# Closing a softmax in column halves and moving the output projection behind it, in a hand-ordered attention stage

## The chip, the cores and the metric

The kernel runs on one core of a Trainium2 chip. The metric is device time in microseconds (us), the median over runs. A core has five engines that run side by side and meet at semaphores: TensorE (PE in the profile; its weight loads are PEld), VectorE (DVE), ScalarE (ACT), GpSimd (POOL) and SyncE (SP, which issues DMAs).

## The reference, cut to what matters

The program is a network of four layers on 2708 tokens of 256 features. The change concerns one part of layer 2, a causal attention ahead of a mixture of experts:

```
h = rmsnorm(x, ln1_w)
q, k, v = h @ wq.T, h @ wk.T, h @ wv.T          # 4 query heads, 2 key/value heads, 64 wide
q, k = rope(q), rope(k)
scores = q @ k.T / 8 ; scores = where(causal, scores, -1e30)
y = softmax(scores) @ v
x = x + y @ wo.T                                # the output projection
flat = rmsnorm(x, ln2_w)
probs = softmax(flat @ router_w.T)              # the two best of 8 experts per token
out = sum over the two experts of weight * (silu(flat @ w1.T) * (flat @ w3.T)) @ w2.T
x = x + out
```

## The kernel before, in words

`attention` cuts the 2708 query columns into six blocks (`cols`): five of 512 (n = 0 to 4) and one of 148 (n = 5). Keys come in tiles of 128. A block has two pairs of heads, p = 0 and p = 1; both key/value heads of a pair are worked on side by side in the two halves of the partitions. In the last block both pairs are done as one, with m = 2 and 296 columns in all. One *step* (n, p, j) is a block, a pair and a key tile j. Causality lets block n see 4(n+1) key tiles, so that early pairs are short: 4, 8, 12, 16 and 20 steps. Two steps make a *group*.

What a step does:
- `scores` (L1913): TensorE multiplies queries and keys into a PSUM tile `sc`, two of which exist. ScalarE takes the exponential of it into an SBUF tile `e` (L1922); the first `e` of a pair is the tile `sum`. There are four `e` tiles. On the diagonal VectorE multiplies a 128-column part by a triangle, `upper` (L1928).
- `values` (L1938), one group later: TensorE adds `V` times `e` into the PSUM tile `po` of the pair, and VectorE adds `e` to `sum` (L1944).
- `close`, once per pair, one group after its last `values`: TensorE sums `sum` over the partitions with a matrix of ones into a PSUM tile `pd` (L1952), VectorE takes the reciprocal of all 512 columns into `yt` (L1954) and multiplies it by `po` (L1955).

Two generators run beside these steps and hand out work in pieces:
- `projects` (`heads`) prepares the next block: normalised rows `f` (VectorE, L124), their transposes `tp` (L1857, copied by ScalarE into `ft`), the values `pv`, and keys and queries in three pieces `pj` (L1884), each followed by two VectorE products with the rotation table (L1887) and an add on POOL (L1888). Behind the last block it frees its pool and starts the loads of the experts' weights. A counter `at` paces it: some 18 steps' worth of pieces per step of the block.
- `sends` (`tails`) takes up a block when both its pairs are closed (`closed`), one block after the other: two token tiles at a time it multiplies `yt` by `wo` into `wy` (the matmul at L139, in `matmul_k`; per tile one product for each pair), adds the normalised row to it (`xa`, L1970), adds that to the residual X on POOL (L1971), squares it on ScalarE (L1973), scales it (`h`, L1978), transposes it, computes the router's logits `pr`, and then, in `route.chunk`, picks the two experts of each token (a chain of small VectorE operations that ends in `dtaken` and `dso_far`), ranks the tokens with two small matmuls `rank` (L1569, L1570), and scatters each row to its two experts with indirect DMAs on POOL's queue (L1590), eight per block of 512 columns.

The PSUM tiles `tp`, `pv`, `pj`, `pd`, `wy`, `pr` and `rank` all come from one pool, `aux`, with two buffers. A piece that needs a buffer waits for whoever last reads what is in it.

TensorE's order is written out by hand (`manual_schedule`): it takes its instructions in the order in which the Python loop below issues them. The other engines' orders come from a scheduler. Per group the loop issues the scores of the group, one piece of `sends`, the values of the group before, the closes that are due, and then pieces of `projects` until the counter is satisfied:

```python
                for step in group:
                    exp = scores(*step)
                next(tails, None)
                for step in before:
                    values(*step)
                ...
                for n, p in ending:
                    close(n, p)
                ...
                while group and at[2] * ... < at[1] * 18:
                    at[2] += 1
                    next(heads, None)
```

After the last close the experts' stage (`mixture`, in `experts`) follows. Its matmuls (`h` at L2125) take the rows that the scatters have placed.

Of the kernel before, what the change touches and what calls it, by code (L numbers as in the profile page):

```python
# [12 lines left out]
ALU = mybir.AluOpType  # L13
# [3 lines left out]
P = 128  # L17
# [18 lines left out]
def rows(t):  # L36
    return min(P, N - t * P)
# [11 lines left out]
def tiles_of(start, length):  # L49
    return range(start // P, (start + length + P - 1) // P)  # L50
# [282 lines left out]
def inverse_root(net, pool, v, scale, eps, name, out=None):  # L333


    nc = net.nc
    n = v.shape[1]
    x = pool.tile([P, n], F32, name=f"{name}x")
    nc.vector.tensor_scalar(x, v, scale, eps, ALU.mult, ALU.add)
    half = pool.tile([P, n], I32, name=f"{name}h")  # L340
    nc.vector.tensor_scalar(half, x.bitcast(I32), 1, None, ALU.logical_shift_right)
    y = pool.tile([P, n], F32, name=f"{name}y") if out is None else out
    nc.vector.tensor_scalar(y.bitcast(I32), half, -1.0, float(0x5F3759DF), ALU.mult, ALU.add)
    t = pool.tile([P, n], F32, name=f"{name}t")
    for _ in range(3):
        nc.vector.scalar_tensor_tensor(t, y, -0.5, y, ALU.mult, ALU.mult)
        nc.vector.tensor_tensor(t, t, x, ALU.mult)
        last = nc.vector.scalar_tensor_tensor(y, t, 1.5, y, ALU.add, ALU.mult)
    return y if out is None else last
# [1436 lines left out]
def attention(net, route, ln2, router, weights, mixture):  # L1786
# [7 lines left out]
    nc, tc, a, X = net.nc, net.tc, net.a, net.X  # L1794
# [3 lines left out]
    with ExitStack() as ctx:  # L1798
# [39 lines left out]
        queries, results = {}, {}  # L1838
# [51 lines left out]
        def by_pairs(t, m, iw):  # L1890

            return t[..., : m * iw].rearrange("p (m i) -> p m i", m=m)
# [4 lines left out]
        outs, sums, es = {}, {}, {}  # L1897
# [48 lines left out]
        def close(n, p):  # L1946
            iw = cols[n][1]
            m = queries[n][p].shape[1]
            e = sums.pop((n, p))
            pd = aux.tile([P, 512], F32, name="pd", tag="aux")  # L1950
            for g, b in enumerate(halves):
                nc.tensor.matmul(pd[b, : m * iw], net.ones[:, :DH], e[:, g, : m * iw], start=True, stop=True)  # L1952
            y = results[n][:, p : p + m, :iw]
            nc.vector.reciprocal(y, by_pairs(pd, m, iw))  # L1954
            nc.vector.tensor_tensor(y, y, by_pairs(outs.pop((n, p)), m, iw), ALU.mult)  # L1955

        def send(n, rp, aux, tag="aux"):
            i0, iw = cols[n]
            its = tiles_of(i0, iw)
            yt = results.pop(n)  # L1960
            ss = rp.tile([P, 4], F32, name="ss")
            nc.vector.memset(ss, 1.0)
            xs, hs = {}, {}
            for k, t in enumerate(its):
                r = rows(t)
                po = aux.tile([P, D], F32, name="wy", tag=tag)
                net.matmul_k(po[:r], yt[:, :, k * P : k * P + r], wo)
                xa = xs[t] = rp.tile([P, D], F32, name="xa", bufs=len(its))
                net.normed(xa, t, ln)
                nc.vector.tensor_tensor(xa[:r], po[:r], xa[:r], ALU.add)  # L1970
                nc.gpsimd.tensor_tensor(X[:r, t, :], X[:r, t, :], xa[:r], ALU.add)  # L1971
                h = hs[t] = rp.tile([P, D + 2], F32, name="h", bufs=len(its) + 1)
                nc.scalar.activation(h[:r, :D], xa[:r], AF.Square, accum_out=ss[:r, k : k + 1])  # L1973
                if k % 2 or tag != "aux":
                    yield
            for k, t in enumerate(its):
                r, h = rows(t), hs[t]
                nc.vector.tensor_tensor(h[:r, :D], xs[t][:r], ln2[:r], ALU.mult)  # L1978
            if tag != "aux":
                yield  # L1980

            root = inverse_root(net, rp, ss, 1.0 / D, 1e-6, "rr")
            yield
            for k in range(0, len(its), 2):
                pair = its[k : k + 2]
                ps = aux.tile([P, 2, 2 * P], F32, name="tp", tag=tag)
                for m, t in enumerate(pair):
                    r, h = rows(t), hs[t]
                    for c in range(2):
                        nc.tensor.transpose(  # L1990
                            ps[:, c, m * P : m * P + r], h[:r, c * P : (c + 1) * P], net.ident[:r, :r]
                        )
                nw = (len(pair) - 1) * P + rows(pair[-1])
                ht = rp.tile([P, 2, 2 * P], F32, name="ht")
                nc.scalar.copy(ht[:, :, :nw], ps[:, :, :nw])
                yield
                pr = aux.tile([P, 2, 8], F32, name="pr", tag=tag)
                for m, t in enumerate(pair):
                    r = rows(t)
                    net.matmul_k(pr[:r, m, :], ht[:, :, m * P : m * P + r], router)  # L2000
                for m, t in enumerate(pair):
                    r = rows(t)
                    nc.vector.tensor_scalar(
                        route.logits[:r, t, :], pr[:r, m, :], root[:r, k + m : k + m + 1], None, ALU.mult
                    )
                yield
            for k, t in enumerate(its):
                r, h = rows(t), hs[t]
                nc.vector.tensor_scalar(h[:r, :D], h[:r, :D], root[:r, k : k + 1], None, ALU.mult)
            yield from route.chunk(rp, aux, its[0], len(its), hs.__getitem__, tag=tag)  # L2010
# [8 lines left out]
        def projects():  # L2019
            for n in range(1, len(cols)):  # L2020
                while at[0] + 1 < n:
                    yield
                yield from (last_project if n + 1 == len(cols) else project)(n)
                ready.append(n)
                yield

        def sends():
            for n in range(len(cols) - 1):
                while n not in closed:
                    yield  # L2030
                yield from send(n, rp, aux)

        ready, closed, ending, at = [0], [], [], [0, 0, 0]
        with tc.manual_schedule(engines={mybir.EngineType.PE}):
            for _ in project(0):
                pass
            steps = [
                (n, p, j)
                for n, (i0, iw) in enumerate(cols)
                for p in range(2 if n + 1 < len(cols) else 1)  # L2040
                for j in range(tiles_of(i0, iw)[-1] + 1)
            ]
            groups = [steps[k : k + 2] for k in range(0, len(steps), 2)]
            heads, tails, before = projects(), sends(), []
            for group in groups + [[]]:
                while group and group[-1][0] not in ready:
                    next(heads)
                if group and group[0][0] > at[0]:
                    at[:] = group[0][0], 0, 0
# [4 lines that stand above are left out]
                    values(*step)  # L2054
                if at[0] + 1 == len(cols):
                    next(tails, None)
                for n, p in ending:
                    close(n, p)
                    if p + 1 == len(queries[n]):
                        closed.append(n)  # L2060
                ending = [(n, p) for n, p, j in before if j == tiles_of(*cols[n])[-1]]
                at[1] += 1
                while group and at[2] * len(queries[at[0]]) * (tiles_of(*cols[at[0]])[-1] + 1) < at[1] * 18:
                    at[2] += 1
                    next(heads, None)
                before = group
            for n, p in ending:
                close(n, p)
            for _ in tails:
                pass  # L2070
# [379 lines left out]
```

## Time and profile before

| what | value |
|---|---|
| median of 3 runs | 2646.69 us (2646.11 to 2649.6) |
| profiled execution, its own time | 2647.78 us |
| its span, first to last instruction | 2646.0 us |
| mean granted clock of TensorE | 0.962 |
| attention stage | about 1560 to 1945 us from the span's start |
| experts of layer 2 | from about 1945 us |
| reciprocals of closes, L1954 | 10 of 512 columns (3350 ns), 1 of 296 (2007 ns) |

The profile's windows give the busy time of each engine in a stretch of the span, with the granted TensorE clock; a matmul of the program appears as two passes in the trace, so `x8` at `wy` is two token tiles. The list of waits says who waited for whom: total us, number of waits, longest. In the timeline each row is a run of like instructions with its start and its length; idle time before it and what ended it stand in brackets. A group of instructions "by form" has the shape, the count, the busy time in us and the mean in ns.

### The profile page before, as it was taken

How to read it: one execution, taken by the hardware profiler on the slowest of the kernel's cores; microseconds unless marked ns; L12 is line 12 of the kernel's file. 1: busy time of each engine (PE TensorE's matmuls, PEld its weight loads, DVE VectorE, ACT ScalarE, POOL GpSimd, SP SyncE). 2: the span in 40 equal slices, each digit the busy share in tenths (PEclk: the TensorE clock that was granted, in tenths of full speed). 3: DMA queues.
4: the chain of work that ended last, by engine and by line, in shares of the span. 5: the costliest groups of instructions: out<-in, count | busy, mean ns of one | idle time of the engine just before them, and what ended most of it. 6: DMA issues, size and time to landing. Idle time of an engine off the chain costs nothing. (4 is left out here: it accounts for less than half of the span.)

```text
span 2646.0 us, 32568 instructions
## 1 busy us (share of the span) xinstructions
PE 2446.7 (92%) x11676; PEld 1581.2 (60%) x11676; DVE 1476.4 (56%) x3258; ACT 1060.2 (40%) x1714; POOL 329.2 (12%) x445
## 2 busy tenths in 40 slices
PE   5999999887999998979799989999899999969998
PEld 4666765574333334468578854444357777747887
DVE  7754348544788886333545457787653222264556
ACT  3444443313787772321434323334422222234454
POOL 1000002100000001134130011222231111110002
PEclk9999999978999999989899999999989999989999
DMA  8899520000000002774310010000231111050001
GB/s 289 281 299 320 172 86 31 3 6 1 1 1 1 1 1 82 170 193 144 91 62 1 1 38 9 19 17 17 101 128 50 33 33 33 22 203 7 1 1 43
DMA packets 106875, 197.70 MB, mean 75 GB/s; under 512 B 8846, under 2 KB 63736, under 8 KB 103876
## 3 DMA queue, kind: packets, MB, share of 16 engines
q1 hardware_dynamic: 88010, 146.82, 17.8%
q0 software_dynamic: 14896, 43.89, 5.1%
q10 hardware_dynamic: 3806, 4.85, 0.6%
q8 instruction: 98, 1.61, 0.3%
q14 instruction: 65, 0.53, 0.1%
HBM read 135.82 MB, written 59.71 MB: 74 GB/s over the span
## 5 line engine op out<-in xcount | busy, mean ns | idle before, releaser
L701 DVE SCALAR_TENSOR_TENSOR e<-e,mask 128x768 f32<-128x768 f32 (+3 forms) x352 | 417.0, 1215 | 241.9 <-ACT e L700 239.1
L700 ACT ACTIVATE e<-big_p,minus_one,ratio 128x768 f32<-128x768 f32 (+3 forms) x352 | 418.6, 1226 | 285.2 <-PE acc L1371 196.8
L1371 PE MATMUL acc<-V,e 128*128 128x257 f32 x1848 | 405.3, 382 | 5.7 <-DVE e L701 5.6
L1371 PEld LDWEIGHTS acc<-V,e 128*128 128x128 f32 x1848 | 352.7, 191 | 58.6 <-issue 7.0
L2125 PE MATMUL h<-w,ft 128*128 (+1 forms) x752 | 233.9, 452 | 1.3 <-DVE yl L1955 1.3
L307 PE MATMUL acc<-F,e 128*128 128x257 f32 (+1 forms) x924 | 212.5, 383 | 3.7 <-DVE e L303 3.4
L836 PE MATMUL acc<-e,V 128*64 128x512 f32 (+1 forms) x1056 | 209.1, 548 | 2.2 <-DVE e L701 2.2
L307 PEld LDWEIGHTS acc<-F,e 128*128 128x128 f32 (+1 forms) x924 | 171.6, 189 | 56.6 <-DVE e L303 29.2
L2142 DVE TENSOR_TENSOR hh<-hh,h 128x682 f32<-128x682 f32 x47 | 40.7, 865 | 243.7 <-PE h L2125 243.7
L2125 PEld LDWEIGHTS h<-w,ft 128*128 128x128 f32 x752 | 135.8, 191 | 57.2 <-issue 1.8
L836 PEld LDWEIGHTS acc<-e,V 128*64 128x64 f32 x1056 | 73.7, 138 | 151.3 <-issue 146.1
L1922 ACT ACTIVATE e<-sc 128x1024 f32<-128x1024 f32 (+4 forms) x131 | 107.1, 863 | 139.2 <-PE sc L1913 116.6
L303 DVE TENSOR_TENSOR e<-e,mask 128x512 f32<-128x512 f32 (+2 forms) x132 | 80.5, 621 | 141.3 <-ACT e L296 139.6
L1944 DVE TENSOR_TENSOR sum<-sum,e 128x1024 f32<-128x1024 f32 (+4 forms) x131 | 135.2, 1032 | 40.1 <-ACT e L1922 19.6
L296 ACT ACTIVATE e<-score 128x512 f32<-128x512 f32 (+2 forms) x132 | 69.4, 544 | 170.4 <-PE score L294 145.1
L2157 PE MATMUL po<-w,ht 114*128 (+1 forms) x564 | 131.5, 383 | 0.9 <-DVE ht L2150 0.9
L1913 PE MATMUL sc<-qt,kt 64*128 64x512 f32 (+5 forms) x568 | 123.9, 555 | 1.4 <-ACT sum L1922 0.9
L2157 PEld LDWEIGHTS po<-w,ht 114*128 114x128 f32 x564 | 107.6, 192 | 23.0 <-DVE ht L2150 8.2
L847 PE MATMUL den<-e,low 128*3 128x512 f32 (+1 forms) x1056 | 117.7, 542 | 0.0
L294 PE MATMUL score<-QK 128*128 128x512 f32 (+2 forms) x264 | 112.0, 553 | 3.4 <-ACT e L296 3.0
L1938 PE MATMUL po<-e,V 128*64 128x512 f32 (+5 forms) x524 | 111.2, 543 | 1.7 <-DVE e L1928 1.7
L2151 ACT COPY ht<-pt 114x256 f32<-114x256 f32 x47 | 17.5, 372 | 201.0 <-DVE ht L2150 201.0
(652 smaller groups left out, 3408.4 us busy)
## 6 DMA issues: line engine op xcount, KB each, us to landing
row<-in_adj SPq DMA_DIRECT2D x21, 1354.0 KB
raw<-in_adjT SPq DMA_DIRECT2D x35, 768.0 KB
hs<-zero SPq DMA_DIRECT2D x8, 2838.0 KB
hidden<-hr SPq DMA_DIRECT2D x32, 256.0 KB
wd<-in_f_wd SPq DMA_DIRECT2D x8, 1024.0 KB
kept<-mask SPq DMA_DIRECT2D x21, 338.5 KB
mask<-kept SPq DMA_DIRECT2D x21, 338.5 KB
w<-in_d_w1T SPq DMA_DIRECT2D x8, 682.0 KB
```

The costliest lines, as they stand in the source:

```text
L294: nc.tensor.matmul(ps[:r, :iw], QK[:, 0, span(j)], QK[:, 1, i0 : i0 + iw], start=True, stop=True)
L307: ended = nc.tensor.matmul(acc[k], e[:r, k * P : (k + 1) * P], F[:r, j, :], start=j == 0, stop=j == NT - 1)
L700: nc.scalar.activation(v, big_p[:, i], AF.Relu, bias=net.minus_one, scale=ratio)
L701: return nc.vector.scalar_tensor_tensor(v, v, 1.0, net.mask[:, j, i], ALU.add, ALU.mult)
L836: nc.tensor.matmul(acc[n][half, :iw], V[:, j, h, :], e[n][:, k, :iw], start=j == 0, stop=j == NT - 1)
L847: nc.tensor.matmul(den[g : g + Q, :iw], low[:, j, h, Q - 1 - q : 2 * Q - 1 - q], e[n][:, k, :iw], start=False, stop=j == NT - 1 and q == Q ...
L1371: nc.tensor.matmul(acc[k][:ri], e[:, k * P : k * P + ri], V[:, j, :], start=j == 0, stop=j == NT - 1)
L1913: nc.tensor.matmul(by_pairs(ps[:r, g], m, iw)[:, :, o:], kt[b, span(j)], qt[b, :, o:iw], start=True, stop=True)
L1938: nc.tensor.matmul(by_pairs(outs[n, p][b], m, iw)[:, :, o:], V[:r, j, g, :], by_pairs(e[:r, g], m, iw)[:, :, o:], start=j == 0, stop=j == ...
L1944: nc.vector.tensor_tensor(total, total, by_heads(e[:r], m, iw)[:, :, :, o:], ALU.add)
L2125: last = nc.tensor.matmul(halves[s, n][:, q, :HALF], fts[s][:, c, :], weights.w13[n][:, es[s], c, q * HALF : (q + 1) * HALF], start=c == 0 ...
L2157: last = nc.tensor.matmul(po, ht[:KP, k, :], w2[:KP, es[s], k, :], start=k == 0, stop=k == KC - 1)
```

## The change

Three edits, all in `attention`:
- `close` takes the reciprocal and the product in two column halves of 256 where m is 1. Where m is 2 it stays one piece.
- `sends` lets two of its turns pass after a block is closed, before it issues the first output projection. In the last block of the loop it has two turns per group, otherwise one.
- The pacing loop of `projects` is left early while `quiet` is above 0, that is in the group of a close and in the one after it, except while block 0 is worked on. Pieces held back are caught up afterwards, since the counter goes on.

```diff
@@ close
-            y = results[n][:, p : p + m, :iw]
-            nc.vector.reciprocal(y, by_pairs(pd, m, iw))
-            nc.vector.tensor_tensor(y, y, by_pairs(outs.pop((n, p)), m, iw), ALU.mult)
+            po = outs.pop((n, p))
+            half = 2 * P if m == 1 else iw
+            for i in range(0, iw, half):
+                y = results[n][:, p : p + m, i : i + half]
+                nc.vector.reciprocal(y, by_pairs(pd, m, iw)[:, :, i : i + half])
+                nc.vector.tensor_tensor(y, y, by_pairs(po, m, iw)[:, :, i : i + half], ALU.mult)
@@ sends
                 while n not in closed:
                     yield
+                for _ in range(2):
+                    yield
                 yield from send(n, rp, aux)
@@ the loop
-            heads, tails, before = projects(), sends(), []
+            heads, tails, before, quiet = projects(), sends(), [], 0
...
+                quiet -= 1
                 for n, p in ending:
                     close(n, p)
+                    quiet = 2
                     if p + 1 == len(queries[n]):
                         closed.append(n)
...
                 while group and at[2] * len(queries[at[0]]) * (tiles_of(*cols[at[0]])[-1] + 1) < at[1] * 18:
+                    if quiet > 0 and at[0]:
+                        break
                     at[2] += 1
                     next(heads, None)
```

## The prediction

> **What bounds the kernel now.** I read the windows first (busy time by stretch), then TensorE's waits inside the attention stage, then the timeline around one close, then the groups by form.
>
> ```profile
> PE 2446.7 (92%) x11676; PEld 1581.2 (60%) x11676; DVE 1476.4 (56%) x3258; ACT 1060.2 (40%) x1714; POOL 329.2 (12%) x445
> ...
> 1560.00:1945.00 385.00, 353.72 (x1634) 155.28 (x1633) 275.76 (x561) 142.06 (x211) 87.48 (x83) 0.95 0.11 36
> 1945.00:2160.00 215.00, 214.81 (x945) 157.08 (x946) 70.28 (x217) 46.36 (x107) 33.57 (x58) 0.99 0.19 63
> ```
>
> The second row is the stage changed, the third the expert stage behind it. TensorE (first number pair) works 354 of 385 us in attention, with a mean clock of 0.95, and without a gap afterwards; VectorE, 276 us, is next. So TensorE's issue order bounds the stage, and only its idle time, and the slow clock that follows it, can be won.
>
> ```profile
> PE wy L139 <- DVE yt L1955: 11.6, 4, 3.4
> PE pj L1884 <- DVE yt L1954: 5.9, 2, 3.6
> PE pj L1884 <- DVE xa L1970: 5.4, 1, 5.4
> ...
> PE pv L139 <- DVE xa L1970: 1.1, 1, 1.1
> ...
> DVE xa L124 <- POOL X L1971: 5.9, 1, 5.9
> ```
>
> Six gaps, 11.6 + 5.9 = 17.5 us, end with a reciprocal or its product: four where the output projection `wy` reads `yt`, two where a projection piece `pj` needs the PSUM tile that `pd` holds. The next two, 6.5 us, end with `xa`, because VectorE itself sat 5.9 us behind POOL. One close, that of query block 2, pair 1, in the timelines:
>
> ```profile
> 1718.85 1.03 PE L1952 MATMUL pd<-sum,ones 128*64 128x512 f32 x4
> 1719.81 0.66 PE L1857 MATMUL tp<-ident,f 128*128 128x128 f32 x4
> 1720.39 1.99 PE L1913 MATMUL sc<-qt,kt 64*128 64x512 f32 x8
> 1722.31 0.70 PE L139 MATMUL wy<-wo,yt 128*128 128x256 f32 x2
> 1725.82 2.23 PE L139 MATMUL wy<-wo,yt 128*128 128x256 f32 x6 [2.81 <-DVE yt L1955]
> 1727.98 2.91 PE L1938 MATMUL po<-e,V 128*64 128x512 f32 x8
> ```
> ```profile
> 1720.75 3.35 DVE L1954 RECIPROCAL yt<-pd 128x512 f32<-128x512 f32 x1
> 1724.02 1.16 DVE L1944 TENSOR_TENSOR sum<-sum,e 128x1024 f32<-128x1024 f32 x1
> 1725.09 0.68 DVE L1955 TENSOR_TENSOR yt<-yt,po 128x512 f32<-128x512 f32 x1
> ```
>
> `pd` ends at 1719.81 (call it T). The reciprocal starts at T+0.94, its product ends at T+5.96, and `wy` arrives at T+2.5. After the gap six passes took 2.23 us where an undisturbed `wy` takes 1.56, and the next `po` 2.91 for 1.94: another 1.64 us. By the same reading the six gaps (2.23, 2.36, 2.81, 3.40, 3.58, 3.13) are followed by 0, 1.83, 1.64, 2.86, 1.61 and 1.64 us of slow matmuls, 9.6 together, and the two POOL gaps (6.5) by 1.9. Removable at most: 17.5 + 9.6 + 8.4 = **35.5 us**.
>
> **What the Trainium skill says.** "TensorE: Matmul & The Clock Gate", Part 1: an idle window of about 3.4 us halves the array's clock, and it takes as long to return. The trace agrees on the halving, but 2.36 us of idle already cost 1.83; the measurement decides. The same page (engine queue depths) calls VectorE a strict FIFO: above, the product waits behind a `sum`. "Perfetto Trace Analysis", Optimizing Scalar/DVE Operations, advises breaking up an instruction that causes bubbles elsewhere, and puts some 125 ns of overhead on each with PSUM. That advice needs the pieces to be consumed separately; below they aren't.
>
> **The change part by part.**
>
> ```profile
> L1954 DVE RECIPROCAL yt<-pd 128x512 f32<-128x512 f32 x10 | 33.5, 3350 | 0.0
> ...
> L1954 DVE RECIPROCAL yl<-pd 128x296 f32<-128x296 f32 x1 | 2.0, 2007 | 0.7 <-PE pd L1952 0.7
> ```
>
> *Halves.* From the two rows, (3350 − 2007)/216 = 6.22 ns a column and 167 ns fixed; 256 columns cost 1759. The product (675 at 512, 461 at 296) is 421 for 256. A close pays 2 × (1759 + 421) − 4025 = 335 ns more, ten closes 3.35 us of VectorE; the last block (m = 2) has one piece and is unchanged. In the built program VectorE issues both half reciprocals and then both products, nothing between. So the first half of `yt` is ready at about T+0.94+3.4+0.4 = T+4.8, the second at T+5.2: against T+5.96 above little is won, and the `sum` adds of the next pair, which used to slip in between, come about 1.0 us later. By itself this part is worth between −0.3 us a close (product no longer behind a `sum`) and +0.3: I take 0. Its cover is TensorE's own work; where VectorE is late this is lost.
>
> *Output projection two groups later.* A group is 8 `sc` and 8 `po` passes, 1.92 + 1.87 = 3.8 us. Two of them put `wy` at T+9 or beyond, past T+5.2: at blocks 0, 2 and 3 its wait goes. In the last block a group takes 1.19 + 1.15, and `wy` moves by one: `wy` reaches its second matmul at about T+4.0 and waits till T+4.3. All of `send` moves along: per block 4 POOL adds of X, 4 squares on ScalarE, the routing chain, and 8 indirect DMAs on POOL's queue (about 1.3 us each, 10.4 in all). On SP's queue only the experts' weight loads behind the last projection move, some 8 us later against close (4,0); 80 us lie between that close and the experts, so I take 0, and up to 8 if that cover were gone. In the built order `rank` of block 0 now stands some 18 us of TensorE work ahead of block 1's `wy` instead of 2 groups: the 8 DMAs are through before the X adds queue, so the POOL gap (8.4 us) goes; I leave 0.5 for a `rank` that arrives as its chain ends.
>
> *No pieces beside a close.* `pj` no longer asks for `pd`'s buffer at T, so the waits of 2.36 and 3.58 go. Pieces are caught up in twos: at block 0/1, `tp`, `tp`, `pv`, `pj` stand in a row (0.3 us for ScalarE's copies). New orders to pay for, none seen in the trace of before:
> - close (0,1): `po` of the diagonal needs VectorE's `upper` behind the reciprocals: T+5.6 against T+4.5, 1.1 us.
> - close (1,0): `wy` of block 0 now stands just ahead. VectorE has `xa`, `h` (behind ScalarE) and next `xa` (behind POOL) before the reciprocal, which I put 2.5 us late: 3.5 us idle and slow matmuls of the size above. Between 0.7 and 5.5; I take 3.7.
> - close (2,0): `wy` one `sc` after `pd`, its second tile in `pd`'s buffer: T+4.4 against T+2.9, 1.5 us.
> - close (3,0): as (1,0), but it shows through the four `e` buffers: 0 to 5; I take 1.5.
> - close (4,0): second half of a `pj` behind `rank`'s buffer, 1.1; close (3,1): 0.3.
>
> The sum, us won: (0,1) 2.23 − 1.1 = 1.1; (1,0) 4.2 − 3.7 = 0.5; POOL gap 8.4 − 0.5 = 7.9; (2,0) −1.5; (2,1) 4.45; (3,0) −1.5; (3,1) 6.26 − 0.3 = 6.0; (4,0) 5.2 − 1.1 = 4.1. From (4,1) to the experts' first `tp` there are 44.5 us: 4.8 go with the gap, 0.3 stays, and the last 8 scatters, now one group nearer to the end, hold the experts' first load by up to 1: 4.2 taken. Together 25; I take off 3 for short waits in 8 reordered stretches that I can't place: **−22 us**. The stage behind starts earlier by the same amount: its TensorE has no gap, and its weight loads begin when attention's buffers close.
>
> The profiled execution took 2647.78 us (span 2646.0 and 1.8 around it), 1.1 above the median 2646.69. 2647.8 − 22 = 2625.8; for a median, **2625**.
>
> **Rivals.**
> - *VectorE's lag eats half.* In the sum the closes (1,0), (2,0), (3,0) keep 3.7 + 1.5 + 1.5 = 6.7 us of stall. If each costs 3.5 us idle and 1.7 slow, that is 15.6, 9 more: about −13, 2634. For it: VectorE is 72% busy in this stage, more beside `send`. Against it: close (2,0) and (3,0) had no gap before.
> - *Nothing moves.* The tight order only shifts waits to `rank` and `wy` slots: 2646. Against it: behind the closes (1,1), (2,0) and (3,0) stand `sc` and `po`, with at most a `tp` or `pr` between, as behind nearly all closes after the change, and TensorE had no gap there.
> - *Slower: the exp buffers.* ScalarE can't write the seventh `e` of a pair before VectorE has added the fourth, and `sc` can't go on before ScalarE has read its tile. From T: the add must end by about T+6.5; with the halves it ends at 0.94 + 4.2 + 1.14 = T+6.3, where before it was T+5.4. If the reciprocal starts later than T+1.1 at most closes, each us of lateness is a us of TensorE, and a slow clock comes with it. It ends slower by 5 once the ten closes lose over 3.4 us each (22 won + 6.7 counted + 5.3 = 34), that is with a lag over 2 us at every one: 2652 and up. Against it: at nine of the ten closes the reciprocal started 0.4 to 0.95 us after `pd`, once 1.6.
> - The change does what it says in the built order, the halves excepted, which is counted.
>
> **How the numbers follow.** 0.2% is 5.3 us, about what a measurement here tells from no change. Main case (−15 to −30): 0.68. Half eaten (−6 to −15): 0.18. Within 5.3: 0.06. Slower: 0.08. So faster 0.86. The range takes all but the last two and the unplaced rest: −34 (nearly all of 35.5) to −6, 2613 to 2641.
>
> **What would show it.** Right: no wait of `wy` on `yt` but in the last block; no `xa` wait of 5 us behind POOL; attention's clock at 0.98 or more; TensorE's idle time in the stage down from 31 to some 15 us; twenty reciprocals of 256 columns at about 1760 ns. Wrong: `po` or `sc` waiting on `upper` or `e` for over 2 us after most closes, or `rank` on `dtaken`.

## The result, and the profile after

The changed kernel took **2629.41 us** (median of 4 runs, 2627.47 to 2632.82) against 2648.07 for the kernel before on the same chip: a ratio of 0.9931, 95% interval 0.9919 to 0.9943. The forecast was 2625 in a range of 2613 to 2641. So the size came out near: 18.7 us won where 22 were forecast. The way there was not the one that I had described. In the profiled execution attention itself won about 31 us, and some 12 of them were given back in the first microseconds of the experts. (A second profiled execution, shown below, won 28 and gave back 2.)

The page's line of engines for the changed kernel, and then its windows; the columns of the rows are as before (TensorE, weight loads, VectorE, ScalarE, POOL, granted clock, DMA share, GB/s):

```profile
PE 2429.3 (93%) x11676; PEld 1575.1 (60%) x11676; DVE 1476.3 (56%) x3278; ACT 1060.7 (40%) x1714; POOL 326.6 (12%) x445
```
```profile
1560.00:1925.00 365.00, 338.96 (x1633) 150.17 (x1632) 275.69 (x583) 142.17 (x210) 85.00 (x83) 0.98 0.13 47
1925.00:2140.00 215.00, 214.29 (x940) 156.47 (x941) 69.97 (x215) 46.52 (x108) 32.56 (x57) 0.98 0.15 47
```

The stretch from the `wq` pieces of block 1 to the experts' first `h` is 19.0 us shorter (370.4 before, 351.3 after), with the same number of passes and the same work on VectorE. In the stage as a whole TensorE's busy time fell from 353.7 to 339.0 us for that work, and the mean clock rose from 0.95 to 0.98: this is slow clock that went. TensorE is still idle for 26 of the 365 us. Its waits in that stretch (total, number, longest):

```profile
PE tp L132 <- DMA f<-hs: 12.8, 1, 12.8
PE wy L139 <- DVE yt L1957: 3.2, 1, 3.2
PE rank L1569 <- DVE dtaken L1560: 2.2, 1, 2.2
PE pj L1884 <- DVE drank L1572: 2.0, 1, 2.0
PE po L1938 <- DVE e L1928: 1.9, 3, 0.8
```

The four waits of `wy` (11.6 us), the two of `pj` on `yt` (5.9) and the two on `xa` (6.5) are all gone. The 3.2 us of `wy` are new: they stand at close (2,0), where the kernel before had no gap. New too, and larger than any wait of the kernel before, is the first row: the experts' first transpose waits for the rows that the scatters have placed. The close of block 2, pair 1, once more in TensorE's and VectorE's timelines:

```profile
1708.11 1.03 PE L1952 MATMUL pd<-sum,ones 128*64 128x512 f32 x4
1709.07 1.99 PE L1913 MATMUL sc<-qt,kt 64*128 64x512 f32 x8
...
1711.97 1.94 PE L1938 MATMUL po<-e,V 128*64 128x512 f32 x8
```
```profile
1710.01 3.36 DVE L1957 RECIPROCAL yt<-pd 128x256 f32<-128x256 f32 x2
1713.29 0.69 DVE L1958 TENSOR_TENSOR yt<-yt,po 128x256 f32<-128x256 f32 x2
```

No idle time stands in brackets in TensorE's rows, and `po` takes the undisturbed 1.94 us where it took 2.91.

Now the seam to the experts in the timelines, with rows of POOL, of the queues of ScalarE and SP, and of TensorE. First the kernel before, then the changed one (in a row of a queue the second number is the time over which its DMAs were issued):

```profile
1935.90 1.51 POOL L1590 DMA_INDIRECT hs<-h,dto  x1 [0.30 <-DMA hs<-h,dto]
1940.75 1.31 ACTq L1712 DMA_DIRECT2D f<-hs  x3
1942.36 6.82 SPq L1460 DMA_DIRECT2D w<-in_d_w3T  x8
1942.99 0.66 PE L132 MATMUL tp<-ident,f 128*128 128x128 f32 x2 [0.18 <-DMA f<-hs]
```
```profile
1911.76 0.97 POOL L1590 DMA_INDIRECT hs<-h,dto  x1 [0.30 <-DMA hs<-h,dto]
1911.91 15.44 SPq L1460 DMA_DIRECT2D w<-in_d_w3T  x8
1917.82 1.34 ACTq L1712 DMA_DIRECT2D f<-hs  x3
1924.91 0.66 PE L132 MATMUL tp<-ident,f 128*128 128x128 f32 x2 [12.78 <-DMA f<-hs]
```

Before, the order was: last scatter, rows `f`, then the experts' weights `w3`. After, the weights are issued 0.15 us behind the last scatter and 5.9 us ahead of the first rows, because attention's buffers, which they go into, close just then: in all nine profiled executions with this order of loads they were issued 0.15 to 0.16 us after `so_many`, the last matmul of attention, began. The rows could be fetched only 6.1 us after the last scatter's issue, and needed 7.1 us to land, where they had needed 2.2. From 1912 to 1925 us the core's DMA engines were busy for 95% of the time (27% from 1905 to 1912). My theory from here on: **the weight loads get ahead of the scatters and of the rows**, and this costs what attention's last part had gained.

### The profile page after: what moved, and what is told of

The parts are those of the page before. It is cut to its first block, busy times and chain, and to the rows that moved or that the text cites. A ratio compares the mean times of both kernels' runs of the same rounds, so it can differ in the third digit from the quotient of the medians.

```text
span 2625.8 us, 32580 instructions
## 1 busy us (share of the span) xinstructions
PE 2429.3 (93%) x11676; PEld 1575.1 (60%) x11676; DVE 1476.3 (56%) x3278; ACT 1060.7 (40%) x1714; POOL 326.6 (12%) x445
```

## The experiments

One table holds them all. Each row is one profiled execution and the median of its kernel, in us. *Start* is where the 16 passes of `wq` pieces for block 1 begin (1574.54 before): it is ahead of all that the change touches, and differed by up to 9 us between executions, so stages are compared by their lengths and not by their places, and the total of one execution can lie far from the median. *A* runs from there to the `rank` of block 4; *B* from there to `so_many` (L1605), the last matmul of attention; *lead* is how long before `so_many` the last scatter was issued; *wait* is TensorE's wait for the experts' first row; *C* runs from `so_many` to the experts' first `h`. With the delay A holds one group of the last block more and B one less, 2.35 us by the passes in the rows.

| kernel | start | A | B | lead | wait | C | median |
|---|---|---|---|---|---|---|---|
| before | 1574.5 | 349.5 | 18.2 | 6.3 | 0.2 | 2.7 | 2648.1 |
| halves | 1583.5 | 342.6 | 15.8 | 3.6 | 0.8 | 2.7 | 2639.7 |
| delay | 1577.5 | 332.7 | 13.4 | 1.3 | 8.8 | 10.4 | 2639.8 |
| quiet | 1581.8 | 339.7 | 14.3 | 2.3 | 7.5 | 9.1 | 2644.5 |
| halves, quiet | 1575.1 | 335.9 | 18.3 | 6.4 | 0.2 | 2.7 | 2633.9 |
| halves, delay | 1580.7 | 335.0 | 12.0 | -0.9 | 13.7 | 15.2 | 2639.5 |
| delay, quiet | 1579.4 | 323.4 | 10.3 | -2.2 | 15.4 | 17.0 | 2631.4 |
| all three (changed) | 1574.8 | 325.1 | 12.0 | 0.0 | 12.8 | 14.3 | 2629.4 |
| changed, again | 1576.3 | 325.1 | 14.5 | 2.6 | 2.9 | 4.5 | 2624.9 |
| before, rows first | 1579.6 | 349.5 | 15.8 | 3.6 | 1.6 | 3.2 | 2648.9 |
| changed, rows first | 1577.5 | 326.7 | 10.3 | -2.2 | 7.3 | 8.9 | 2626.7 |
| delay, quiet, rows first | 1575.5 | 323.3 | 12.0 | -0.1 | 5.3 | 6.9 | 2622.6 |
| the same, again | 1575.4 | 323.4 | 10.3 | -2.2 | 7.2 | 8.8 | 2621.1 |

From the first `h` to the end all thirteen take 698.2 to 702.4 us, in no order that follows the edits.

**Halves alone.** The reciprocal and product of a close in two column halves, the rest as before:

```diff
...
+            half = 2 * P if m == 1 else iw
+            for i in range(0, iw, half):
+                y = results[n][:, p : p + m, i : i + half]
+                nc.vector.reciprocal(y, by_pairs(pd, m, iw)[:, :, i : i + half])
+                nc.vector.tensor_tensor(y, y, by_pairs(po, m, iw)[:, :, i : i + half], ALU.mult)
```

> The kernel before with the reciprocals in two column halves, and nothing else. My theory: a close lasts as long as before on VectorE (two halves in about 3.4 us together, against 3.35 for the whole), so no difference: 0 +- 2 us against the kernel before (2646 to 2650), the six gaps of TensorE in the same places. Rival (VectorE's lag): both halves now stand ahead of the sum adds of the next pair, TensorE waits on e or po, 3 to 9 us slower (2651 to 2657).

Measured: 2639.74 us (2637.46 to 2647.71, 6 runs), ratio 0.9969, interval 0.9956 to 0.9981. Both theories fall: the halves alone are worth about 8 us, and A is 6.9 shorter. (The profiled execution is the slowest of the six, 2647.71: it reached the stage 9 us late, see *start*.) The close of block 2, pair 1 shows how, in TensorE's and VectorE's timelines of this run:

```profile
1730.95 0.70 PE L139 MATMUL wy<-wo,yt 128*128 128x256 f32 x2
1733.08 1.56 PE L139 MATMUL wy<-wo,yt 128*128 128x256 f32 x6 [1.44 <-DVE yt L1958]
1734.58 1.94 PE L1938 MATMUL po<-e,V 128*64 128x512 f32 x8
```
```profile
1729.39 3.36 DVE L1957 RECIPROCAL yt<-pd 128x256 f32<-128x256 f32 x2
1732.67 0.68 DVE L1958 TENSOR_TENSOR yt<-yt,po 128x256 f32<-128x256 f32 x2
```

`pd` ends at 1728.45 (T) and `wy` goes on at T+4.6, where the kernel before had it at T+6.0: the first token tiles need only the first half of `yt`, and nothing stands between reciprocal and product. The gap shrinks from 2.81 to 1.44 us, and no slow pass follows: six passes of `wy` take 1.56 us (2.23 before), `po` 1.94 (2.91). That is 1.4 us of idle and 1.6 of clock at one close. Over A the four waits of `wy` fall from 11.6 to 7.3 us and TensorE's busy time from 323.8 to 321.0: 7.0 together, near the 6.9 measured. The fall of the waits follows from the order; how much of the slow clock would go in another execution is not shown, since the same gap is not always followed by slow passes (last section).

**Delay alone.** Two lines, from the kernel before:

```diff
+                for _ in range(2):
+                    yield
                 yield from send(n, rp, aux)
```

> The kernel before with the output projection two turns later, and nothing else. My theory: the four wy gaps (11.6 us and some 6 of slow clock) and the 5 us wait on xa go, attention gets shorter by 18 to 24 us; but the last eight scatters are one group nearer to the end of attention, so that the experts' weight loads get ahead of them, and TensorE's first wait in the experts is 10 to 13 us: net -7 to -13 us (2635 to 2641). Rival (that wait comes from the whole program being earlier, not from the delay): attention shorter by as much, first wait of the experts under 3 us, net -18 to -24 (2624 to 2630).

Measured: 2639.81 us (7 runs), ratio 0.997, interval 0.9957 to 0.9983. A and B together are 21.7 us shorter and the experts' first wait is 8.8, with C 7.7 longer. My theory's stage numbers hold for attention and nearly for the wait, and against the rival the median lies 10 us above its range. By itself that does not say what the wait comes from.

**Quiet alone.**

```diff
+                    quiet = 2
...
+                    if quiet > 0 and at[0]:
+                        break
```

> The kernel before with no projection pieces beside a close, and nothing else. My theory: the two pj gaps (5.9 us and about 3.5 of slow clock) go, less up to 3 us for new orders; the last scatters stand where they stood before, so the experts' first row load is not held (under 1 us): net -5 to -10 us (2638 to 2643), all of it kept. Rival 1 (wy stands beside the close as before, and takes over the pj gaps): within 3 us of before. Rival 2 (the wait at the experts comes with any shorter attention): attention shorter by 5 to 10 and the wait takes most of it back, within 3 us of before.

Measured: 2644.48 us (20 runs), ratio 0.9986, interval 0.9979 to 0.9993. A is 9.8 us shorter, so rival 1 falls. That this is near what the two `pj` gaps and their slow clock hold (9.4) is in part luck: TensorE's idle time in A fell by only 3.8 us (the `pj` waits of 5.9 go, but the waits of `wy` grow from 11.6 to 12.7, and a new one of `tp` on `drank` takes 1.8), and 6.0 are busy time, that is slow clock. My "not held" was wrong too: the wait was 7.5 us, and C grew by 6.3 where A and B together had won 13.7. The scatters stood in their old place, but B happened to last 14.3 us instead of 18.2, so that the lead shrank to 2.3. The median lies just above my range, and 3.8 us under the kernel before, just outside rival 2's. It is the lead that matters and not which edit shortens it, and the delay is only one of the things that change it.

**Delay and quiet, whole reciprocals**, from the changed kernel:

```diff
-            for i in range(0, iw, half):
...
+            y = results[n][:, p : p + m, :iw]
+            nc.vector.reciprocal(y, by_pairs(pd, m, iw))
+            nc.vector.tensor_tensor(y, y, by_pairs(outs.pop((n, p)), m, iw), ALU.mult)
```

> The changed kernel with whole reciprocals again (delay and quiet kept). My theory: the halves do nothing, within 2 us of the changed kernel (2627 to 2632). Rival (the halves let wy start on the first half of yt, or shorten the product's wait behind a sum): 5 to 10 us slower than the changed kernel (2634 to 2640). Other rival (VectorE's lag): 3 to 7 us faster (2622 to 2627).

Measured: 2631.38 us (4 runs), ratio 0.9933, interval 0.9917 to 0.995, within 2 us of the changed kernel. Yet it is not true that the halves do nothing: A is 1.7 us *shorter* without them (3.4 us less idle time, 1.5 more busy time). In this execution B was shorter as well, so the last scatter was issued 2.2 us after attention's end, and the first wait grew to 15.4 us. The total hides both.

**Halves and delay.** To see whether the halves still help where the delay has taken `wy`'s waits away. From the changed kernel:

```diff
-                    if quiet > 0 and at[0]:
-                        break
```

> The kernel before with halves and delay, without quiet. My theory: halves help only where wy waits for yt, and the delay takes those waits away; attention (from the wq pieces of block 1 to so_many) stays at 344 to 348 us (346.0 with the delay alone), total as with the delay alone within 3 us (2637 to 2643). Rival (the gain of the halves alone, 9.2 us of attention, is added): attention at 336 to 338, total 2631 to 2634.

Measured: 2639.47 us (11 runs), ratio 0.9965, interval 0.9956 to 0.9975; the stage from the `wq` pieces to `so_many` 346.9 us. My theory's numbers hold, the rival's (336 to 338) don't.

**Halves and quiet.** From the changed kernel:

```diff
-                for _ in range(2):
-                    yield
```

> The kernel before with halves and quiet, without delay. My theory (halves help only where wy waits for yt, and here it waits at four closes): the four waits fall from 12.8 us (quiet alone) to 7 to 9, attention from 354.0 (quiet alone) to 344 to 348. Rival (the 9.2 us of the halves alone came from the pj closes or from chance): attention stays at 352 to 356. The rows at the experts' start are held by 10 us or more in either case (7.5 with quiet alone, longer when attention ends earlier).

Measured: 2633.86 us (4 runs), ratio 0.9938, interval 0.9917 to 0.9959. The waits of `wy` fall from 12.8 to 8.5 us and A from 339.7 to 335.9, as expected; but the stage as a whole was 354.2 us, in the rival's range, because B took 18.3. The last sentence of the expectation missed altogether: with a lead of 6.4 us nothing was held, the rows came as in the kernel before, and so a *longer* attention than in the first execution of the changed kernel, by 17 us, cost only 7.2 in the total of the two executions (4.5 between the medians).

So the halves are worth 6.9 us of A alone, 3.8 beside quiet, and cost 2.3 beside the delay (one execution each). Beside both, three executions with halves took 325.1 to 326.7 us and three without 323.3 to 323.4. They help where `wy` waits for `yt`. Where it doesn't, they hold back VectorE's other work: with them `po` waits 0.80 us at close (0,1) and 0.74 at (1,0) for the product with `upper`, without them at neither, and the wait at (2,0) is 3.19 us with and 2.18 without.

**The rows ahead of the weights.** The `w3` loads are moved behind the first two row loads, which go to the same queue; nothing else is changed:

```diff
         core.close()
-        weights.more()
         mixture(exp, lambda *work: send(len(cols) - 1, *work))
...
-                fetch(s, (nc.scalar if s < 3 else nc.gpsimd) if cut else None)
+                fetch(s, (nc.sync if s < 2 else nc.scalar if s == 2 else nc.gpsimd) if cut else None)
+                if cut and s == 1:
+                    with tc.issue_after(route.loaded.ins):
+                        weights.more()
```

> The changed kernel with the experts' w3 weight loads issued behind the first two row loads (which go on the same queue) and not ahead of them; nothing else. My theory (the weight loads get ahead of the last scatters and of the rows): the last scatters land within some 2.5 us and the rows within some 2.5 more, TensorE's first wait in the experts falls from 12.8 to 4 to 6 us, some 7.8 us faster than the changed kernel: 2619 to 2625 against 2629.4. Rival (the scatters themselves come too late, whatever else is loaded): the wait stays over 10 us, within 2 us of the changed kernel. Second rival (w3 is needed soon): the first wait falls, but TensorE waits for w as long a little later, within 2 us again.

Measured: 2626.69 us (5 runs), ratio 0.9919, interval 0.9905 to 0.9933. The seam of its profiled execution:

```profile
1916.72 0.97 POOL L1590 DMA_INDIRECT hs<-h,dto  x1 [0.30 <-issue]
1919.36 0.82 SPq L1712 DMA_DIRECT2D f<-hs  x2
1920.86 7.09 SPq L1460 DMA_DIRECT2D w<-in_d_w3T  x8
1922.28 0.66 PE L132 MATMUL tp<-ident,f 128*128 128x128 f32 x2 [7.35 <-DMA f<-hs]
```

The rows landed 2.9 us after their issue instead of 7.1, and the last scatter let them go after 2.6 instead of 6.1, both as the theory has it. The first wait fell to 7.3 and not to 4 to 6, since in this execution B was 1.7 us shorter and the scatter came 2.2 us after attention's end. C is 5.4 us shorter; the median moved by 2.7, less than the 7.8 forecast, and the intervals overlap, so that by the total alone this order is not shown to be faster. By the wait the first rival (over 10) falls; the second is not needed: the stretch behind `h` is no longer than in other kernels. The rows also changed their queue here; the second execution of the changed kernel, below, bears on that.

**The control**, the same order of loads in the kernel before:

> The kernel before with the new order of loads and nothing else, a control. My theory: before, the last scatter was issued 6.3 us ahead of attention's end and the first rows held TensorE by 0.2 us, so there is nothing to win: 0 +- 2 us against the kernel before (2646 to 2650). Rival (the order of loads is worth something by itself, wherever the scatters stand): 5 to 8 us faster (2640 to 2643).

Measured: 2648.87 us (13 runs), ratio 0.9998, interval 0.9989 to 1.0006. The order of loads shows no gain where the scatters come early.

**Delay, quiet and rows first, without halves:**

> The same order of loads, with whole reciprocals (delay and quiet kept). My theory: attention is some 3 us shorter than with the halves, as in the run without halves (333.7 us against 337.0), but the last scatter is then issued some 2 us after attention's end, so most of it is given back: within 3 us of the run with halves and the new order of loads (2618 to 2627). Rival (attention's 3 us stay): 3 to 5 us faster than that run.

Measured: 2622.55 us (2620.63 to 2626.14, 5 runs), ratio 0.991, interval 0.9896 to 0.9924. That is 4.1 us faster than with the halves, outside my 3 us and in the rival's range, though the two intervals overlap: A was 3.5 us shorter in the profiled executions and this stayed, since in this one B was 1.7 us longer and the scatter was out by attention's end.

**The changed kernel and that one, side by side:**

> The changed kernel as it is, on the same chip as the next run, so that the two can be compared: 2627 to 2632 by every theory.

> Delay and quiet, whole reciprocals, w3 loads behind the first two row loads, a second time and beside the changed kernel. By my theory 5 to 9 us faster than it (2620 to 2626), with the first wait of the experts at 5 to 6 us. If the 6.9 us between the medians of the earlier runs were chance, within 3 us of it.

Measured: 2624.91 us (2619.26 to 2632.18, 6 runs; ratio 0.9914, interval 0.9894 to 0.9934) and 2621.07 us (2620.51 to 2621.21, 5 runs; ratio 0.9893, interval 0.9876 to 0.991). Both expectations missed: the changed kernel came out below its 2627 to 2632, and the difference of 3.8 us lies between the 5 to 9 of my theory and the 3 of chance, with a first wait of 7.2 us in place of 5 to 6. The two intervals overlap, so the advantage is likely rather than settled. The more telling result is the changed kernel itself. Its profiled execution, at 2622.12 us, was 5.3 faster than the first one, at 2627.47, with the same A to 0.02 us. Its seam:

```profile
1913.34 0.97 POOL L1590 DMA_INDIRECT hs<-h,dto  x1 [0.30 <-DMA hs<-h,dto]
...
1915.24 0.72 PE L1952 MATMUL pd<-sum,ones 128*64 128x296 f32 x4 [3.22 <-issue]
...
1915.95 1.38 ACTq L1712 DMA_DIRECT2D f<-hs  x3
1916.05 7.64 SPq L1460 DMA_DIRECT2D w<-in_d_w3T  x8
1919.24 0.66 PE L132 MATMUL tp<-ident,f 128*128 128x128 f32 x2 [2.86 <-DMA f<-hs]
```

TensorE stood still for 3.22 us ahead of the last `pd`, for a reason that the profile doesn't show, and B was 2.6 us longer. That was enough for the last scatter to land and for the rows to be issued 0.10 us ahead of the weights. The wait fell from 12.78 to 2.86 us. A longer attention, in the same kernel, went with a faster program. The rows were on ScalarE's queue here, as in the first execution, and still took only 3.3 us: it is the order at the seam that counts, and not the queue.

Over all thirteen executions the rows took 2.2 to 3.3 us from issue to use where they were issued ahead of `w3` (eight executions), and 6.4 to 7.9 where behind it (five). The last scatter let the rows go 2.6 to 3.3 us after its issue where `w3` came at least 1.4 us behind it, and 6.1 to 7.1 where `w3` came within 0.2 us or ahead. (In the kernel before and with halves and quiet, leads of over 6 us, the rows were held by attention's own last steps.) Between a lead of 2.3 us (quiet) and 2.6 (changed, again), where the rows just went ahead of `w3`, the first wait falls from 7.5 to 2.9. Whether the small transfers stand behind the large ones in a queue or share the DMA engines with them, these runs don't tell apart.

## Why the prediction was right or wrong

**What bounds the kernel: right.** Only TensorE's idle time and slow clock were there to win, and both fell: from the `wq` pieces to `so_many`, idle from 28.9 to 12.4 us and busy from 338.7 to 324.6.

**The sum up to `rank` of block 4: too small by 4.6.** Counted with the moved group, A won 24.5 + 2.35 = 26.8 us, against 22.2 (the terms add up to 25.2, less 3 for unplaced waits). Term by term, the measured column being TensorE's idle time:

| term | forecast, us left | measured |
|---|---|---|
| (0,1), `upper` behind the reciprocals | 1.1 | 1.2 |
| (1,0), `wy` of block 0 just ahead | 3.7 (0.7 to 5.5) | 0.74 |
| POOL gap | 0.5 | 0 |
| (2,0), `wy` one `sc` after `pd` | 1.5 | 3.2 |
| (3,0) | 1.5 (0 to 5) | 0.43 |
| (4,0), `pj` behind `rank`'s buffer | 1.1 | 2.0 |

(1,0) was put too high: the reciprocal started at T+1.5, not 2.5 or more. (2,0) was put too low: there the reciprocal started at T+2.7, behind a slow `sum`. The rest nearly cancels, so the 3 us for unplaced waits were not needed. Both executions of the changed kernel have these waits alike within 0.01 us.

**Halves at 0: wrong in its working.** The working had the right times for the first half of `yt` and set the difference aside as "little"; it also took the pieces not to be consumed separately, and they are: `wy` went on at T+4.6. Alone, 1.1 us a wait at four waits and the clock behind them are 6.9 us. In the whole change they cost 1.7 us (3.5 with the rows first), near 0 for another reason: the delay takes away the waits that the halves shorten. The added 335 ns of VectorE a close was wrong too, see below.

**Delay and quiet: right, and additive.** Alone they shorten A by 16.8 + 2.35 = 19.2 and by 9.8; together by 28.5 of 29.0 (profiled executions, slow clock included). The POOL gap went as forecast.

**B: not in the sum.** It won 6.2, of which 2.35 is the moved group; the other 3.9 is not explained. B took 14.5 in the second execution of the changed kernel, 2.6 more, and 15.8 instead of 18.2 in the control, so that much of it can be chance.

**The seam: the step that failed.** "The last 8 scatters, now one group nearer to the end, hold the experts' first load by up to 1", and the weight loads "begin when attention's buffers close", taken as no cost. The place was right, the price was wrong: C grew by 11.6 us in the first execution, by 1.8 in the second. With the delay or quiet and the old order of loads it grew by 6.3 to 14.3 in four kernels, and by nothing with halves and quiet, where the lead was 6.4 us. What I missed is that the two meet. When attention's end comes close behind the last scatter, or ahead of it, the loads that start with that end get ahead of the scatters that have not landed and of the rows. With the rows first C is 4.2 to 6.2 over the kernel before; with a lead of 6 us it doesn't grow.

So 25 (a seam of under 1 in it) less 3 gave 22; the runs gave 26.8 + 3.9, less 11.6 at the seam, plus 1.4 from the stretch behind the first `h`, less 0.2 for a later start: 20.3, the difference of the spans (20.2). In this execution the forecast was near because two errors of opposite sign met, attention's gain put too low and the seam's cost put too low: that was luck. In the second one they hardly met, 26.8 + 1.3 less 1.8, plus 1.1, less 1.7 for the start, and it won 25.6. The rivals fell: no lag ate half, and `e` cost at most 0.8 us at any close.

**The signs that I named.** Clock 0.98: yes. No long `xa` wait: yes. Idle at 15: 12.4 up to `so_many`, but 26 with the seam. Twenty reciprocals of about 1760 ns: yes, 1721. `wy` without a wait on `yt` but in the last block: no, 3.2 at (2,0). `rank` on `dtaken` over 2 us, named as a sign of wrong: 2.2, and 1.7 before already.

## What to carry to other kernels

When a stage gets shorter, look at what starts with its end and what must be finished by then: bulk loads that were harmless behind late small transfers get ahead of them, and the gain is paid back at the seam. Measure a stage by its own length between two fixed instructions, and in more than one execution, since a total can hide a gain and its loss. Two cures for one wait don't add up: a piecewise result helps only as long as a consumer waits for the first piece.

## What was not expected of the hardware

- Two half reciprocals, 1721 ns each in the trace, take 3.36 us back to back, as long as the whole one (3350 ns): 82 ns of their sum overlaps, so that halving cost VectorE nothing there.
- A VectorE add took far longer than its usual 1.2 us at close (2,0): the two rows below are the timelines of VectorE and POOL in the changed kernel; two adds needed 4.34 us while POOL added beside them. This made the reciprocal late. The same pair takes 3.43 us there in the run with whole reciprocals and 2.56 at close (2,1). That POOL's add is the cause was not tested.

```profile
1672.65 4.34 DVE L1944 TENSOR_TENSOR sum<-sum,e 128x1024 f32<-128x1024 f32 x2 [2.25 <-PE po L1938]
```
```profile
1673.29 1.28 POOL L1888 TENSOR_TENSOR qt<-qt,tmp 128x512 f32<-128x512 f32 x1
```

- Idle time of TensorE and slow clock are not tied by the length of a gap. The same `pj`, the one of the term (4,0) above, after the same gap, was followed by slow passes in the changed kernel with the rows first and by none in the changed kernel (second execution; the first is alike):

```profile
1850.73 0.77 PE L1884 MATMUL pj<-ft,wq 128*128 128x148 f32 x4 [1.98 <-DVE drank L1572]
1851.43 2.90 PE L1913 MATMUL sc<-qt,kt 64*128 64x512 f32 x8
```
```profile
1849.50 0.77 PE L1884 MATMUL pj<-ft,wq 128*128 128x148 f32 x4 [1.98 <-DVE drank L1572]
1850.20 1.99 PE L1913 MATMUL sc<-qt,kt 64*128 64x512 f32 x8
```

  The next `po` took 2.67 and 1.94 us; together these 1.64 us are nearly the whole difference in A between the two (326.7 and 325.1). Likewise 3.40 us at close (3,1) cost 2.86 us of slow clock in the kernel before and nothing in the run with quiet alone. The Trainium skill ("TensorE: Matmul & The Clock Gate", Part 1) speaks of windows of about 3.4 us that run freely, so that where work falls in them counts; that fits, but no run here shows the windows, and a gap of 1.98 us is shorter than one. A price for slow clock at a single gap, as in the prediction, is therefore good only on average.
